# Layer 2's last block by quarters of the tokens, its anchors with the weights held in the array, and the last layer's weights turned in layer 0

## The chip, the cores and the metric

The kernel runs on one core of a Trainium2 chip. The core has a matrix engine (TensorE, PE in the profile; its weight loads are shown apart as PEld), a vector engine (VectorE, DVE), a scalar engine (ScalarE, ACT), GpSimd (POOL) and a queue engine (SyncE, SP), which here issues nearly all of the DMAs. Each engine works through its own queue in order. They meet through semaphores. The metric is the device time of one execution in microseconds (us). The time before is the median of three runs; the profile is of one more execution.

## What is computed

The reference chains four layers over 1024 tokens of 512 features, each as `x = x + ffn(cond(x))`. All is f32.

```python
x = x + _L0_ffn_ref(_L0_cond_ref(x, ...))   # gated FFN with LoRA, then top-2 of 8 LoRA experts
x = x + _L1_ffn_ref(_L1_cond_ref(x, ...))   # adapter pair, then softmax-weighted experts
x = x + _L2_ffn_ref(_L2_cond_ref(x, ...))   # attention over a paged cache, then the block below
x = x + _L3_ffn_ref(_L3_cond_ref(x, ...))   # top-2 experts, then 64 experts, top 16
```

The change rewrites the second half of layer 2, with `x` there the attention's output (called `y2` in the kernel):

```python
def _L2_ffn_ref(x, W, b, A, Bmat, LiMEs):         # A: 512x32, Bmat: 32x512, LiMEs: 8x32
    H = jnp.einsum('btd,od->bto', x, W) + b
    z = jnp.einsum('btd,dr->btr', x, A)
    anchors = jnp.arange(N_GRAM - 1, T, N_GRAM)   # every second token, from token 1
    H_slice = H[:, anchors, :E]
    delta_slice = jnp.einsum('bar,er->bae', z[:, anchors], LiMEs)
    H_scale = jnp.maximum(jnp.max(jnp.abs(H_slice)), EPS)
    d_scale = jnp.maximum(jnp.max(jnp.abs(delta_slice)), EPS)
    logits = ((1.0 - GAMMA) * (H_slice / H_scale) + GAMMA * (delta_slice / d_scale)) / TEMPERATURE
    probs = jax.nn.softmax(logits, axis=-1)
    ...                                           # thresholded and normalised: weights
    p_mix = jnp.einsum('bte,er->btr', jnp.repeat(weights, N_GRAM, axis=1), LiMEs)
    return H + jnp.einsum('btr,ro->bto', z * p_mix, Bmat) * scaling
```

Layer 3 uses, among others, a 512x512 matrix `W` (`base3` in the kernel) and the experts' `B` (`wB3`) in a turned form. Layer 2 uses the product of `A` and `LiMEs` transposed, for which `A` (`A2`) must be turned.

## The kernel before

The 1024 tokens lie in the columns of `x`, a tile of 128 partitions by four chunks of features by 1024 tokens. A block is 128 tokens (eight blocks), a half is 512, a quarter is 256. Every f32 matmul stands as two records in the trace and a transpose on PE as one.

*Order.* The engines' queues come out of a scheduling layer that may move instructions past each other where data allow. `kept(...)` keeps an instruction in program order on its engine. PE's matmuls stand in program order in the parts named here.

*Layer 0* ends (lines 632 to 672) with the down projection: four `Down` objects, one for each half of the tokens `g` and of the outputs `k`, each a list of matmuls `dn` over the inner dimension with VectorE additions `du`, `dp` between (`begin`, `go_on`), then `lora` and `out`. VectorE, POOL and SP have gaps there.

*Layer 2's attention* is `run` (line 1326), a loop of 32 steps `n`. In each step PE makes scores `st` (line 1173), ACT exponentials, PE the weighted values `av` (line 1225). The sums go through `sums` in DRAM: SP writes `sums<-inv` (line 1217) and reads `R<-sums` (line 1218), and VectorE scales `av` by R into `oT` (line 1235). The output projection is the Strassen-like products `wo_one`, `wo_two`, `wo_six` (line 979) over quarters. From `n == 5` on, `end.prepare` (line 1784) builds part of the layer's second half: four PE transposes turn `A2` (`A2Tp`), ACT copies it to `A2T`, and `alp` (line 1794) multiplies it with LiMEs into columns 8 to 15 of `WH`, whose first eight columns are rows of the layer's W. In the last steps the blocks of `y2` are turned on PE (`turn`, `y2T`, line 1812).

*The second half of layer 2* is in `ending` (line 1741). `low` (line 1815) makes z for one half of the tokens: `A2` is held as the weights for 16 matmuls of 128 columns, each block on one of four groups of 32 array columns; VectorE copies it to `zq`. `anchors` (line 1824) makes the logits' two parts `hd`: 128 anchor tokens are the weights (every second column of `y2T`), `WH` (16 columns) streams, eight matmuls a half (two groups of anchors, four chunks of features), and VectorE adds the bias `b16`. `product` (line 1841) makes H for a block: 16 matmuls of 128 columns into one bank `h`. Low and anchors of the first half run at step 30 (lines 1422 to 1424), product of block 0 after step 31 (line 1427), the rest in `layer2` (line 2195). `routing` (line 1855) reduces `hd` to two maxima, takes them over the partitions with the POOL all-reduce `top` (line 1867) and makes the weights `p` on VectorE and ACT. `gains` (line 1904) turns `p` on PE (`pT`), multiplies by LiMEs (`pmix`) and forms `zp = 0.5 z p_mix`. `delta` (line 1928) adds Bmat's product into the open banks of H, 16 matmuls of 128 columns a half, and VectorE adds H to `x`, one block at a time. Between the products `weights_turned` (line 1971) turns layer 3's `base3` (`W3p`, 16 PE transposes, four ACT copies) and `wB3` (`wB3p`, four transposes, one copy), and `fold_scores` (line 1985) multiplies them with router matrices (`qwp`, `qbp`, `fkp`, `gkp`).

*Layer 3* begins with PE's `midp` matmuls (line 53, a helper), which read `x` in order of the blocks. POOL makes sums of weights for its fast products (`Bws`, `W3s`, line 2012). `sums_checked` (line 756) reads the attention's sums back, reduces them on VectorE and over the partitions with POOL's all-reduce `anyone` (line 765), and copies the result to `redo_i` on VectorE; if a sum lies out of its range, a second, general attention would run behind the kernel.

## Time and profile before

| | us |
|---|---|
| runs of before | 1492.9, 1496.06, 1497.18 (median 1496.06) |
| the profiled execution's own time | 1490.35 |
| its span on the core | 1488.6 |
| `av` matmuls (line 1225), busy | 290.8 |
| `st` matmuls against the cache (line 1173), busy | 237.4 |
| `h`, layer 2's product, busy (256 records) | 31.2 |
| the attention's steps, about | 250 to 1350 |
| layer 2's second half, from the last `y2T` to layer 3's first `midp` | 1352.6 to 1389.7 |
| layer 3, to the end | 1389.7 to 1488.6 |

The profiled execution is 5.7 us shorter than the median of the runs, and 1.75 us of it lie around the span. The busy time of a group adds the records' own durations. Matmuls overlap a little, so in a timeline a group's stretch, from its start to the start of the next, is shorter than its busy time. A timeline line gives the start, the busy time, the engine, the line, the operation, what it writes and reads, the shape, how many records, and in brackets the idle time before and what ended it. A line of windows gives, for each stretch, the busy time and the instructions of PE, PEld, DVE, ACT and POOL, then the clock that TensorE was granted (1.00 is full), the DMA engines' share, and GB/s. In the chain of waits each piece has its start, its length and what ran.

### The profile page before, as it was taken

To read this page: it belongs to the slowest core of one execution; us is meant where nothing else is said; L and a number is where in the kernel's file an instruction comes from. 1 tells how busy PE (TensorE), PEld (TensorE's weight loads), DVE (VectorE), ACT (ScalarE), POOL (GpSimd) and SP (SyncE) were. 2 spreads that over 40 slices of the span, in tenths; PEclk is the share of its full clock that TensorE was granted. 3 is DMA by queue.
4 is the path that set the end of the run, shared out by engine and by line. 5 is a ranking of instruction groups with operands and counts; after the bars stand their busy time and mean duration, and the time that the engine had idled before them with its cause. 6 is when DMAs were issued, how large, how long until landed. Compare 5 with 4: busy or idle time off the path is not lost.

```text
span 1488.6 us, 18093 instructions
## 1 busy us (share of the span) xinstructions
PE 1476.6 (99%) x5603; PEld 938.3 (63%) x5603; DVE 1065.6 (72%) x2121; ACT 562.0 (38%) x1422; POOL 856.4 (58%) x876
## 2 busy tenths in 40 slices
PE   9999999999999999999999999999999999999998
PEld 7888787455555655555555555565555555558887
DVE  4665425388888787787778778787878878855475
ACT  1111101044545544454554454454445455431110
POOL 2241104567777777776777777677777777622310
PEclk9999999999999999999999999999999999999999
DMA  7411001213545444564454455345445534433001
GB/s 242 118 44 32 1 1 55 94 36 115 183 148 173 150 119 129 150 183 126 135 152 131 128 158 177 110 135 163 129 125 166 168 106 138 120 104 98 1 9 52
DMA packets 155257, 171.44 MB, mean 115 GB/s; under 512 B 52624, under 2 KB 125776, under 8 KB 155024
## 3 DMA queue, kind: packets, MB, share of 16 engines
q1 hardware_dynamic: 136976, 133.18, 30.0%
q0 software_dynamic: 17056, 36.49, 7.7%
q8 instruction: 47, 0.77, 0.2%
q10 hardware_dynamic: 1120, 0.52, 0.1%
q14 instruction: 58, 0.48, 0.1%
HBM read 129.36 MB, written 40.76 MB: 114 GB/s over the span
## 4 chain that ended last, share of the span: by engine, by line
PE 96%; DVE 2%; ACT 0%; DMA 0%; issue 0%; DVEq 0%; ACTq 0%; SPq 0%
PE st L1173 18%; PE av L1225 18%; PE g L367 9%; PE q_six L979 8%; PE wo_two L979 6%; PE q_one L979 6%; PE q_five L979 6%; PE dn L367 5%; PE wo_six L979 4%; PE wo_one L979 4%; PE eo_l L53 3%; PE z L1761 2%; PE h L1761 2%; PE midp_l L53 1%; PE o L1761 1%; PE gu L367 1%
## 5 line engine op out<-in xcount | busy, mean ns | idle before, releaser
L922 POOL DMA_INDIRECT kn<-in_k_cache,kvrow_k x256 | 272.2, 1063 | 77.1 <-issue 71.2
L922 POOL DMA_INDIRECT vals<-in_v_cache,kvrow_v x256 | 272.3, 1064 | 73.6 <-issue 60.2
L1225 PE MATMUL av<-pT,vals 128*128 128x512 f32 x640 | 290.8, 592 | 0.2 <-DVE oT L1235 0.2
L1177 ACT ACTIVATE pT<-st,hide 128x512 f32<-128x512 f32 x256 | 175.9, 687 | 192.0 <-PE st L1173 178.8
L1173 PE MATMUL st<-qT,kT 128*128 128x512 f32 x512 | 237.4, 596 | 0.0
L1225 PEld LDWEIGHTS av<-pT,vals 128*128 128x128 f32 x640 | 121.4, 190 | 152.7 <-issue 148.3
L1078 POOL TENSOR_TENSOR vq<-q,txq 128x256 f32<-128x256 f32 x128 | 121.1, 976 | 130.6 <-ACT sqq L1052 92.9
L1173 PEld LDWEIGHTS st<-qT,kT 128*128 128x128 f32 x512 | 97.2, 191 | 109.3 <-issue 103.3
L1193 DVE TENSOR_TENSOR part<-pT 128x512 f32<-128x512 f32 x128 | 88.3, 691 | 76.2 <-ACT pT L1177 62.8
L979 PE MATMUL q_one<-q,x 128*128 128x384 f32 x256 | 93.0, 486 | 0.0
L1052 ACT ACTIVATE sqq<-q 128x128 f32<-128x128 f32 x252 | 78.2, 310 | 10.4 <-DVE q L1028 3.8
L979 PEld LDWEIGHTS q_one<-q,x 128*128 128x128 f32 x256 | 48.5, 190 | 39.8 <-issue 14.3
L979 PE MATMUL q_six<-q_s,xs_all 128*128 128x384 f32 x192 | 69.8, 486 | 0.0
L1033 ACT COPY q<-q_one 128x256 f32<-128x256 f32 x32 | 11.9, 372 | 151.9 <-PE q_one L979 133.5
L979 PE MATMUL wo_one<-o,oT 128*128 128x256 f32 x256 | 65.9, 380 | 1.1 <-ACT k L1033 0.8
L1173 PE MATMUL st<-qT,kTn 128*128 128x512 f32 x128 | 65.4, 592 | 0.0
L979 PE MATMUL wo_two<-o_s,os 128*128 128x256 f32 x256 | 60.6, 379 | 0.3 <-DVE os L938 0.3
L1177 ACT ACTIVATE pT<-st,rs 128x512 f32<-128x512 f32 x64 | 44.0, 687 | 38.5 <-PE av L1225 18.5
L979 PEld LDWEIGHTS wo_one<-o,oT 128*128 128x128 f32 x256 | 48.5, 190 | 15.0 <-issue 1.9
L436 POOL TENSOR_TENSOR ws<-wu 128x256 f32<-128x256 f32 (+1 forms) x9 | 6.4, 711 | 86.8 <-DMA wu<-in_WuT 79.8
L1209 ACT COPY rows<-rows 32x32 f32<-32x32 f32 x96 | 20.7, 216 | 92.1 <-DVE rows L1204 91.4
L367 PE MATMUL g<-xs,ws 128*128 128x256 f32 (+1 forms) x240 | 55.1, 379 | 0.0
(461 smaller groups left out, 2838.5 us busy)
## 6 DMA issues: line engine op xcount, KB each, us to landing
turned_new<-qkt SPq DMA_DIRECT2D x120, 160.0 KB
turned_cached<-kt SPq DMA_DIRECT2D x128, 128.0 KB
kT<-turned_cached SPq DMA_DIRECT2D x32, 512.0 KB
R<-sums SPq DMA_DIRECT2D x32, 512.0 KB
qT<-turned_new SPq DMA_DIRECT2D x30, 512.0 KB
q<-in_WqT SPq DMA_DIRECT2D x8, 1024.0 KB
o<-in_WoT SPq DMA_DIRECT2D x8, 1024.0 KB
kn<-in_k_cache,kvrow_k POOLq DMA_INDIRECT x256
```

The lines of the kernel that those rows point to most:

```text
L53: pe.matmul(o, lhsT, rhs, start=start, stop=stop)
L367: pe.matmul(o, lhsT, rhs, start=start, stop=stop, skip_group_check=True)
L922: kept(pool.indirect_dma_start(out=d[:, c, :], out_offset=None, in_=kc if what == "k" else vc, in_offset=bass.IndirectOffsetOnAxis(ap=kvro ...
L979: kept(pe.matmul(o, l[:, c, :], r[:, c, :], start=start and c == 0, stop=c == 1, skip_group_check=True))
L1052: kept(act.activation(sq, S[n][m][:, j, i, :], AF.Square, accum_out=S[n]["ssq"][:, j, col : col + 1]))
L1078: kept(pool.tensor_tensor(to, t[:, b, :, hi : hi + 64], wx[:, b, lo : lo + 64].unsqueeze(2).to_broadcast(list(to.shape)), ALU.mult,))
L1173: kept(pe.matmul(ps, s["kT"][:, c, 4 * j : 4 * j + 4, :] if c < 4 else s["kn"][:, j], s["qT"][:, :, REP * j : REP * (j + 1), :].rearrange( ...
L1177: kept(act.activation(pT[:, c, :, :].rearrange("p i t -> p (i t)"), ps, AF.Exp, **(dict(bias=hide[:, b, c : c + 1]) if c < 4 else dict(bia ...
L1193: kept(dve.tensor_tensor(o, l, r, ALU.add))
L1209: kept(act.copy(rows[0:32, g, :], rows[32 * g : 32 * g + 32, 0, :]))
L1225: kept(pe.matmul(ps, v[:, c, :], pT[:, c, :, :].rearrange("p i t -> p (i t)"), start=c == 0, stop=c == NC - 1, skip_group_check=True,))
L1761: return pe.matmul(o, lhsT, rhs, start=start, stop=stop, skip_group_check=True)
```

## The change

- *Product by quarters.* `product` takes 256 tokens in one matmul instead of 128: 64 matmuls in all for 128. A bank holds two chunks of outputs for a quarter, so each quarter has two banks. Quarter 0 (was: block 0) stands after step 31, the others in `layer2`.
- *Low and anchors once.* Both run once in `layer2` for all tokens and are gone from step 30. `low` has a quarter of the tokens on each group of 32 array columns, 16 matmuls of 256 columns; ACT copies it. `anchors` holds `WH` as the weights, padded with zeros from 16 to 32 columns (a POOL memset), and streams the anchors of a quarter (128 columns at a stride of two) to each column group, 16 matmuls; VectorE copies the result, `low` runs, and one PE transpose turns it.
- *`pmix`* is four matmuls of 128 columns instead of eight of 64. *`delta`* is 16 matmuls of 256 columns, a quarter on each row group, instead of 32 of 128; quarter 3's delta opens its banks, and product adds to them.
- *Turned weights.* `base3`, `wB3` and `A2` are loaded in layer 0 (six SP DMAs), turned by VectorE in blocks of 32x32, and written to DRAM tensors (24 SP DMAs, pieces of 128 bytes that put each block in its place), in three pairs between the `Down` parts. Later `W3` and `wB3T` are loaded from there in the place of `base3` and `wB3`, and `A2T` at step 5 by an SP DMA. All PE transposes of these three, and the six ACT copies, are gone.

In the order of the engines' queues, the changed kernel has: on SP at step 5, `A2T`'s DMA right behind `R<-sums`; on POOL, both groups of `W3s` sums (eight operations) ahead of the all-reduce `anyone`, where before the second group stood behind it; on VectorE, `x<-h` of quarters 0 to 2 (first bank), then `redo_i`, then `x<-h` of the second banks and of quarter 3; on PE, after the last turns, anchors, z, one transpose, the product of quarter 1 and half of 2, `qwp`, `qbp`, `pT`, `pmix`, the other half of quarter 2, delta, half of quarter 3, `fkp`, `gkp`, the other half, `midp`.

```diff
+    late_weights = [
+        (a["base3"][d * P : (d + 1) * P, :], w3T[:, d * P : (d + 1) * P].rearrange("(b i) (q j) -> q i b j", i=32, j=32))
+        for d in range(DC)
+    ]
+    late_weights.append((a["wB3"], wB3T.rearrange("(b i) (q j) -> q i b j", i=32, j=32)))
+    late_weights.append((
+        a["A2"].rearrange("(c p) r -> p c r", p=P), A2T.rearrange("i (c q j) -> q i c j", q=4, j=32)
+    ))
...
+        def weights_turned():
+            for n in range(0, len(late_weights), 2):
+                ts = []
+                for i, (src, _) in enumerate(late_weights[n : n + 2]):
+                    t = w0.tile([P, 2, D], F32, tag=("Ad", "Bg")[i], name=f"late_{n + i}")
...
+                    kept(sp.dma_start(first if len(src.shape) == 2 else first.rearrange("p (c j) -> p c j", j=src.shape[2]), src))
+                    ts.append((t, m))
+                for (_, dst), (t, m) in zip(late_weights[n : n + 2], ts):
+                    kept(dve.transpose(t[:, 1, :m], t[:, 0, :m]))
+                    for q in range(4):
+                        kept(sp.dma_start(dst[q], t[32 * q : 32 * q + 32, 1, :m].rearrange("i (b j) -> i b j", j=32)))
+                yield
...
-        for d in downs:
-            d.go_on()
+        turning = weights_turned()
+        downs[0].go_on()
+        next(turning)
+        downs[1].go_on()
...
         downs[0].go_on()
+        next(turning)
         mids0, route0, mix0, outs0 = experts("l0", ...)[:4]
...
         downs[1].go_on()
+        next(turning)
...
-            if n + 2 == len(steps):
-                end.low(0, bank)
-                end.anchors(0, bank)
         divided(n)
         every(outputs(n))
-        end.product(0, "st", bank)
+        end.product(0, ("st", "st"), bank)
...
-    WH = early.tile([P, DC, 16], F32, tag="WH", name="WH")
+    WH = early.tile([P, DC, 32], F32, tag="WH", name="WH")
+    kept(pool.memset(WH[:, :, 16:32], 0.0))
...
     def prepare(bank, room):
-        pt = bank("mm", [P, D], "A2Tp")
-        for c in range(DC):
-            kept(pe.transpose(pt[:32, c * P : (c + 1) * P], A2[:, c, :], ident))
         A2T = room([32, D], "A2T")
-        kept(act.copy(A2T, pt[:32]))
+        kept(sp.dma_start(A2T, late_turned[2]))
...
+    def low(bank):
+        ps = bank("mm", [P, NT // 4], "z2")
         for c in range(DC):
-            for j in range(HB):
-                b = g * HB + j
-                mmq(ps[slot(j), :], A2[:, c, :], Y2T[0][:, c, b * P : (b + 1) * P], c == 0, c == DC - 1)
-        dve.tensor_copy(zq[:, g, :], ps)
+            for q in range(4):
+                mmq(ps[slot(q), :], A2[:, c, :], Y2T[0][:, c, quarter(q)], c == 0, c == DC - 1)
+        act.copy(zq, ps)
+
+    def anchors(bank, meanwhile):
+        ps = bank("mm", [P, P], "hdT")
+        for c in range(DC):
+            for q in range(4):
+                mmq(ps[slot(q), :], WH[:, c, :], Y2T[0][:, c, q * NT // 4 + 1 : (q + 1) * NT // 4 : 2], c == 0, c == DC - 1)
+        hdT = L3.w3.tile([P, P], F32, tag="hdT", name="hdTs")
+        dve.tensor_copy(hdT, ps)
+        meanwhile()
+        ps = bank("mm", [P, NA, 32], "hd")
+        pe.transpose(ps.rearrange("p q e -> p (q e)"), hdT, ident)
+        dve.tensor_tensor(hd, ps[:, :, 0:16], b16.unsqueeze(1).to_broadcast([P, NA, 16]), ALU.add)
...
+    def product(q, tags, bank, at=range(2), begun=False):
+        for i, tag in zip(at, tags):
+            ps = H[q, i] if begun else bank(tag, [P, 2, NT // 4], f"h_{q}_{i}")
+            for o in range(2):
+                for c in range(DC):
+                    mmq(
+                        ps[:, o, :], W["2"][:, c, (2 * i + o) * P : (2 * i + o + 1) * P], Y2T[0][:, c, quarter(q)],
+                        not begun and o == 0 and c == 0, begun and c == DC - 1,
+                    )
+            H[q, i] = ps
...
+    def delta(tags, bank):
+        for i, tag in enumerate(tags):
+            H[3, i] = bank(tag, [P, 2, NT // 4], f"h_3_{i}")
+        for i in range(2):
+            for o in range(2):
+                for q in range(4):
+                    at = (2 * i + o) * P
+                    mmq(H[q, i][:, o, :], Bm[slot(q), at : at + P], zp[slot(q), :], q == 3 and o == 0, q < 3)
+
+    def added(q):
+        for i in range(2):
+            t = x[:, 2 * i : 2 * i + 2, quarter(q)]
+            dve.tensor_tensor(t, H[q, i], t, ALU.add)
...
-        L3.base = load("base3", [P, DC, D], chunks(a["base3"]))
+        L3.W = load("W3", [P, DC, D], chunks(late_turned[0]))
...
-        L3.wB = load("wB3", [P, D], a["wB3"])
+        L3.wBT = load("wB3T", [P, DC, P], chunks(late_turned[1]))
...
-    def layer2(y2, bank, held=lambda: None, do=range(NB)):
+    def layer2(y2, bank, do=range(NB)):
         for b in do:
             turn(y2, b, bank)
...
+        anchors(bank, lambda: low(bank))
         where = ["mm"]
+        folding = fold_scores(lambda tag, shape, name: bank(where[0], shape, name))
+        if (0, 0) not in H:
+            product(0, ("st", "st"), bank)
+        product(1, ("st", "av"), bank)
         routing()
+        product(2, ("av",), bank)
+        next(folding)
         gains(bank)
+        product(2, ("mm",), bank, range(1, 2))
+        delta(("mm", "mm"), bank)
+        for q in range(3):
+            added(q)
         where[0] = "st"
+        product(3, ("mm",), bank, range(1), begun=True)
+        next(folding, None)
+        product(3, ("mm",), bank, range(1, 2), begun=True)
+        added(3)
```

More of the change, by code (lines that the diff above doesn't have):

```diff
@@ L67, in forward @@
     x = xpool.tile([P, DC, NT], F32, tag="x", name="x")
+    w3T, wB3T, A2T = (
+        nc.dram_tensor(n, shape, F32, kind="Internal").ap()
+        for n, shape in (("w3_turned", (D, D)), ("wB3_turned", (D, P)), ("A2_turned", (32, D)))
+    )
[7 more added lines that the diff above has]
+    ))
+    late_turned = w3T, wB3T, A2T
     c0 = ExitStack()
@@ L564, in forward @@
         w11 = const.tile([P, 136], F32, tag="w11", name="w11")
+        def weights_turned():
[3 more added lines that the diff above has]
+                    t = w0.tile([P, 2, D], F32, tag=("Ad", "Bg")[i], name=f"late_{n + i}")
+                    m = math.prod(src.shape[1:])
+                    first = t[:, 0, :m]
+                    kept(sp.dma_start(first if len(src.shape) == 2 else first.rearrange("p (c j) -> p c j", j=src.shape[2]), src))
[5 more added lines that the diff above has]
+                yield
         def ranks_to_ranks(wb1T):
@@ L741, in end_of @@
                 lambda shape, name: ww.tile(shape, F32, tag="q7", name=name),
-                lambda shape, name: ww.tile(shape, F32, tag="qs", name=name), room, chunks, mm, in_order,
+                lambda shape, name: ww.tile(shape, F32, tag="qs", name=name), room, chunks, mm, late_turned, in_order,
             )
@@ L788, in forward @@
                 lambda shape, name: ww.tile(shape, F32, tag="q7", name=name),
-                lambda shape, name: ww.tile(shape, F32, tag="qs", name=name), room, chunks, mm,
+                lambda shape, name: ww.tile(shape, F32, tag="qs", name=name), room, chunks, mm, late_turned,
             )
@@ L1741, in ending @@
 def ending(
-    tc, a, out, x, ident, bias3, experts, early, tile_of_w2, tile_of_aw, room, chunks, mm, kept=lambda i: i
+    tc, a, out, x, ident, bias3, experts, early, tile_of_w2, tile_of_aw, room, chunks, mm, late_turned, kept=lambda i: i
 ):
@@ L1780, in ending @@
     kept(sp.dma_start(b16[:, 0:8], a["b8"].partition_broadcast(P)))
-    zq = early.tile([P, TG, P], F32, tag="zq", name="zq")
+    zq = early.tile([P, NT // 4], F32, tag="zq", name="zq")
     hd = early.tile([P, NA, 16], F32, tag="hd", name="hd")
     def prepare(bank, room):
-        pt = bank("mm", [P, D], "A2Tp")
-        for c in range(DC):
-            kept(pe.transpose(pt[:32, c * P : (c + 1) * P], A2[:, c, :], ident))
         A2T = room([32, D], "A2T")
-        kept(act.copy(A2T, pt[:32]))
+        kept(sp.dma_start(A2T, late_turned[2]))
         yield
@@ L1813, in turn, with quarter @@
         (act.copy if b % 2 else dve.tensor_copy)(Y2T[0][:, :, b * P : (b + 1) * P], ps)
-    def low(g, bank):
-        ps = bank("mm", [P, P], f"z2_{g}")
+    def quarter(q):
+        return slice(q * NT // 4, (q + 1) * NT // 4)
+    def low(bank):
+        ps = bank("mm", [P, NT // 4], "z2")
         for c in range(DC):
-            for j in range(HB):
-                b = g * HB + j
-                mmq(ps[slot(j), :], A2[:, c, :], Y2T[0][:, c, b * P : (b + 1) * P], c == 0, c == DC - 1)
-        dve.tensor_copy(zq[:, g, :], ps)
-    def anchors(g, bank):
-        ps = bank("mm", [P, 2, 16], f"hd_{g}")
-        for i in range(2):
-            t0 = (2 * g + i) * 2 * P
-            for c in range(DC):
-                mm(ps[:, i, :], Y2T[0][:, c, t0 + 1 : t0 + 2 * P : 2], WH[:, c, :], c == 0, c == DC - 1)
-        dve.tensor_tensor(
-            hd[:, 2 * g : 2 * g + 2, :], ps, b16.unsqueeze(1).to_broadcast([P, 2, 16]), ALU.add
-        )
+            for q in range(4):
[12 more added lines that the diff above has]
+        dve.tensor_tensor(hd, ps[:, :, 0:16], b16.unsqueeze(1).to_broadcast([P, NA, 16]), ALU.add)
     H = {}
@@ L1839, in shifted @@
             kept(act.activation(x[:, c, :], x[:, c, :], AF.Identity, bias=bcol[:, c : c + 1]))
-    def product(b, tag, bank):
-        ps = bank(tag, [P, DC, P], f"h_{b}")
-        for o in range(DC):
-            for c in range(DC):
-                mmq(
-                    ps[:, o, :], W["2"][:, c, o * P : (o + 1) * P], Y2T[0][:, c, b * P : (b + 1) * P],
-                    o == 0 and c == 0, False,
-                )
-        H[b] = ps
+    def product(q, tags, bank, at=range(2), begun=False):
[6 more added lines that the diff above has]
+                        not begun and o == 0 and c == 0, begun and c == DC - 1,
+                    )
+            H[q, i] = ps
     sm = early
@@ L1911, in gains @@
         act.copy(pT, pt[:8].rearrange("p i t -> p (i t)"))
-        pm = bank("mm", [P, TG, 64], "pmix")
-        for g in range(TG):
-            for j in range(HB):
-                b = g * HB + j
-                mmq(pm[slot(j), g, :], Li, pT[:, b * 64 : (b + 1) * 64], g == 0, True)
-        zp = L3.w3.tile([P, TG, P], F32, tag="zp", name="zp")
+        pm = bank("mm", [P, P], "pmix")
+        for q in range(4):
+            mmq(pm[slot(q), :], Li, pT[:, q * P : (q + 1) * P], True, True)
+        zp = L3.w3.tile([P, NT // 4], F32, tag="zp", name="zp")
         dve.scalar_tensor_tensor(
-            zp.rearrange("p g (t two) -> p g t two", two=2),
-            zq.rearrange("p g (t two) -> p g t two", two=2),
+            zp.rearrange("p (t two) -> p t two", two=2),
+            zq.rearrange("p (t two) -> p t two", two=2),
             0.5,
-            pm.unsqueeze(3).to_broadcast([P, TG, 64, 2]),
+            pm.unsqueeze(2).to_broadcast([P, P, 2]),
             ALU.mult,
@@ L1926, in gains @@
         Z["zp"] = zp
-    def delta(g):
+    def delta(tags, bank):
         zp, Bm = Z["zp"], L3.Bm
-        for o in range(DC):
-            for j in range(HB):
-                mmq(H[g * HB + j][:, o, :], Bm[slot(j), o * P : (o + 1) * P], zp[slot(j), g, :], False, True)
-        for j in range(HB):
-            b = g * HB + j
-            t = x[:, :, b * P : (b + 1) * P]
-            dve.tensor_tensor(t, H[b], t, ALU.add)
+        for i, tag in enumerate(tags):
+            H[3, i] = bank(tag, [P, 2, NT // 4], f"h_3_{i}")
+        for i in range(2):
+            for o in range(2):
+                for q in range(4):
+                    at = (2 * i + o) * P
[4 more added lines that the diff above has]
+            dve.tensor_tensor(t, H[q, i], t, ALU.add)
     def open3(w3, ex_sm):
@@ L1969, in copied @@
         return t
-    def weights_turned(bank):
-        L3.W = L3.w3.tile([P, DC, D], F32, tag="W3", name="W3")
-        for o in range(DC):
-            ps = bank("mm", [P, DC, P], f"W3p_{o}")
-            for d in range(DC):
-                pe.transpose(ps[:, d, :], L3.base[:, d, o * P : (o + 1) * P], ident)
-            copied(None, None, ps.rearrange("p c d -> p (c d)"), L3.W[:, o, :])
-            yield
-        ps = bank("mm", [P, DC, P], "wB3p")
-        for o in range(DC):
-            pe.transpose(ps[:, o, :], L3.wB[:, o * P : (o + 1) * P], ident)
-        L3.wBT = copied([P, DC, P], "wB3T", ps)
     def fold_scores(bank):
@@ L2193, in last @@
             sp.dma_start(out[o * P : (o + 1) * P, tok], t)
-    def layer2(y2, bank, held=lambda: None, do=range(NB)):
+    def layer2(y2, bank, do=range(NB)):
         for b in do:
             turn(y2, b, bank)
-        for g in range(TG):
-            if g or len(do) > HB:
-                low(g, bank)
-                anchors(g, bank)
+        anchors(bank, lambda: low(bank))
         where = ["mm"]
-        def free(tag, shape, name):
-            return bank(where[0], shape, name)
-        turning, folding = weights_turned(free), fold_scores(free)
-        for b in range(HB):
-            if b not in H:
-                product(b, "av" if b == HB - 1 else "st", bank)
-                next(turning, None)
+        folding = fold_scores(lambda tag, shape, name: bank(where[0], shape, name))
+        if (0, 0) not in H:
+            product(0, ("st", "st"), bank)
+        product(1, ("st", "av"), bank)
         routing()
+        product(2, ("av",), bank)
+        next(folding)
         gains(bank)
-        product(HB, "av", bank)
-        next(turning, None)
-        delta(0)
+        product(2, ("mm",), bank, range(1, 2))
+        delta(("mm", "mm"), bank)
+        for q in range(3):
+            added(q)
         where[0] = "st"
-        for b in range(HB + 1, NB):
-            product(b, "mm", bank)
-            for _ in turning:
-                pass
-            next(folding, None)
-        delta(1)
+        product(3, ("mm",), bank, range(1), begun=True)
+        next(folding, None)
+        product(3, ("mm",), bank, range(1, 2), begun=True)
+        added(3)
     def layer3(bank, between=lambda: None):
@@ L2265, in ending @@
     return SimpleNamespace(
-        prepare=prepare, load_w2=load_w2, load_aw=load_aw, turn=turn, low=low, anchors=anchors,
+        prepare=prepare, load_w2=load_w2, load_aw=load_aw, turn=turn,
         product=product, shifted=shifted, open3=open3, layer2=layer2, layer3=layer3,
```

## Prediction

> **What bounds it now.** I read the busy shares first, then the chain of waits, then TensorE's timeline where the change touches it, then the queues that feed those places.

> ```profile
> PE 1476.6 (99%) x5603; PEld 938.3 (63%) x5603; DVE 1065.6 (72%) x2121; ACT 562.0 (38%) x1422; POOL 856.4 (58%) x876
> ```

> ```profile
> PE 96%; DVE 2%; ACT 0%; DMA 0%; issue 0%; DVEq 0%; ACTq 0%; SPq 0%
> ```

> TensorE (PE) is busy for 99% of the span and 96% of the chain. So the sum is: PE time that goes, less PE time that comes, less new PE idle. An f32 matmul is two records, a transpose one; since records overlap I take a group's cost from its start to the next start.

> The parts that are rewritten, and rows for what replaces them:

> ```profile
> 1309.53 0.82 PE L1761 MATMUL z<-y2T,A 128*32 128x128 f32 x6
> ...
> 1313.46 0.66 PE L53 MATMUL hd<-WH,y2T 128*128 128x16 f32 x5 [0.59 <-issue]
> 1313.97 5.38 PE L1173 MATMUL st<-qT,kT 128*128 128x512 f32 x8
> ```

> ```profile
> 1349.48 1.03 PE L979 MATMUL wo_two<-o,os 128*128 128x256 f32 x4
> 1350.34 1.03 PE L979 MATMUL wo_six<-o_s,oT 128*128 128x256 f32 x4
> ...
> 1374.70 3.84 PE L1761 MATMUL h<-y2T,WT 128*128 128x128 f32 x32
> 1378.38 0.60 PE L1982 MATMUL wB3p<-ident,wB 128*128 128x128 f32 x4
> ...
> 1400.48 1.03 PE L1761 MATMUL fp<-AwT,W 128*128 128x256 f32 x4
> 1401.35 1.03 PE L1761 MATMUL fp<-sums,W 128*128 128x256 f32 x4
> ```

> The reader is to see: half of `low` and `anchors` between two attention steps, 1309.53 to 1313.97, with PE idle 0.59 inside; a block of `product`, 32 records of 128 columns in 3.68 us (0.115 each); and records of 256 columns at 0.86/4 and 0.87/4, mean 0.2165.

> **What goes from PE.** The stretch at 1309.53: 4.44. Its second half in layer 2: z 0.34 + 1.30, hd 1.95, together 3.59. Product: 256 records; its stretches in the timeline add up to 30.0. The 16 transposes `W3p` and 4 `wB3p`: 2.53. `delta`: 2.21. `pmix`: 0.36 (8 records of 64 columns at 0.045). `A2Tp` at step 5: 0.44 (495.58 to 496.02). Three idles of layer 2, before wo_one 0.31, wo_two 0.26 (both behind the wait for R, which the longer first quarter, 32 × 0.2165 = 6.93 from 1340.30 to 1347.2, covers) and pT 0.19: 0.76. Sum 44.3.

> **What comes on PE.** Product: 128 records × 0.2165 = 27.7. `low`: 32 records of 32 rows × 256 columns; the nearest rows are layer 0's td, 88 such records from 166.93 to 171.82, 0.0556 each: 1.78. `anchors`: 32 records of 32 rows × 128 columns at stride 2; nothing like it is in the trace; below, z (26 in 1.02, unit stride): 1.25; above, td at its full 0.0556: 1.78; I take 1.5, as the columns are z's and only the stride is new. One transpose 0.12. `pmix`, 8 records of 128 columns: qbp's 8 take 0.33. `delta`: 32 records from 0.0556 (td) to 0.0675 (g<-tgm, 8 in 0.54): 1.8 to 2.2, taken 2.0. Idles: `hdT` is copied by DVE while `low` runs, 1.8 of cover for a copy of some 0.3 and its hand-overs, taken 0.15; `pmix` stands right behind pT, so PE waits for ACT's copy, 0.57 with hand-overs 0.85. With 0.8 at midp (below) the sum is 35.2.

> **Step 5, a new wait.** `prepare` no longer makes A2T on PE but fetches it over SP's queue, behind R<-sums, while `alp` keeps its place on PE:

> ```profile
> 496.02 4.46 PE L1225 MATMUL av<-pT,vals 128*128 128x512 f32 x10
> 500.41 1.05 PE L1794 MATMUL alp<-LiT,A2T 32*128 32x8 f32 x8
> ```

> ```profile
> 499.14 0.32 SPq L1217 DMA_DIRECT2D sums<-inv  x1
> 500.66 0.35 SPq L1218 DMA_DIRECT2D R<-sums  x1
> 501.05 2.09 SPq L1128 DMA_DIRECT2D turned_cached<-kt  x4
> ```

> ```profile
> 1338.35 1.35 DMA sums<-inv
> ...
> 1339.77 3.81 DMA R<-sums
> ```

> SP waits at 500.66 until sums<-inv has landed, so A2T (64 KB) is issued at some 501.05, where now turned_cached starts. PE reaches alp at 500.41 - 0.44 = 499.97 and waits, and all st matmuls of step 6 stand behind alp on PE. The DMA's time is bounded by the nearest rows: 1.52 from issue to release (sums<-inv here, 499.14 to 500.66), landing at 502.57, idle 2.6; and 3.81 (R<-sums, 512 KB, in the chain), landing at 504.86, idle 4.9. I take 4.9: 64 KB in rows of 2 KB behind R on the same rings is nearer to R than to the small write. Behind A2T on SP the four turned_cached issues come 0.35 later; they serve step 7, so nothing waits. ACT's copy of A2T goes.

> Sum: 44.3 - 35.2 - 4.9 = **4.2 us gained**.

> **The clock.** After the stretch with z and hd the granted clock falls:

> ```profile
> 1314.00:1316.00 2.00, 2.00 (x5) 0.96 (x5) 0.20 (x2) 0.06 (x1) 0.00 (x0) 0.53 1.04 403
> 1316.00:1318.00 2.00, 2.00 (x4) 0.72 (x4) 0.00 (x0) 0.98 (x2) 0.00 (x0) 0.62 1.04 377
> ```

> (third to last: clock). The eight st matmuls take 5.21 there and 3.44 elsewhere: 1.77 lost. The change removes that stretch, but PE's new idle before alp may bring a drop of its own. I set the one against the other, net 0; the bounds are +1.77 (the old drop goes, none comes) and -1.77 (the old one stays by other causes, a new one comes).

> [...]

> **Hidden, costed at nothing.** In layer 0 VectorE turns five 128x512 tiles (0.70 each, as STREAM_TRANSPOSE partT 0.706) and one 128x128: 3.7 us in DVE's idles 178.60 to 191.19, 212.76 to 224.67 (11.90) and 233.3 to 242.55. PE's dn matmuls cover them; SP is idle from 132.6 to 243.22, so 6 loads and 24 stores (8 a pair, 0.65 issue each as the two kTn in 1.19 show, 5.2 a pair) fit, the last pair from 234.4 to 239.6, ahead of q<-in_WkT at 243.22. If that cover went, q<-in_WkT would be late, then q_s on DVE (251.42) and eo's add (256.45) behind it; PE needs that bank at 264.8: some 7.7 us of slack. The stores go out in pieces of 128 bytes; the DMA share is near zero there and W3 is wanted 1100 us later. W3 and wB3T take base3's and wB3's place in the load queue with the same bytes. `low`'s copy moves from DVE to ACT, idle there.

> **POOL, and midp.** Now the second group of W3s runs behind the second all-reduce; after the change both stand ahead of it.

> ```profile
> 1359.14 0.37 POOL L1867 PARTITION_ALL_REDUCE top<-big  x1 [25.89 <-DVE big L1863]
> 1366.23 1.40 POOL L2012 TENSOR_TENSOR W3s<-W 128x256 f32<-128x256 f32 x2 [6.71 <-ACT m L1893]
> ...
> 1379.24 0.38 POOL L765 PARTITION_ALL_REDUCE anyone<-some  x1 [5.83 <-issue]
> 1386.32 1.40 POOL L2012 TENSOR_TENSOR W3s<-W 128x256 f32<-128x256 f32 x2 [6.70 <-ACT gk L1968]
> ```

> After an all-reduce POOL is idle 6.7 before its next arithmetic, and 5.83 the other way (1373.41 to 1379.24). In the times of before: layer 2's turns end at 1355.6 (product's quarter is 2.2 longer), hd is ready near 1360, `top` ends near 1360.7; 6.7 later, 1367.4, 16 operations start (0.69 to 0.72, 11.3 together), end 1378.7; 5.83 gives 1384.5; `anyone` 0.38, `redo_i`, and the add x<-h_0_1 (0.62) behind it on DVE: 1385.8. PE: pT 1369.6, pmix 1370.5, product to 1374.3, delta to 1376.3, product 1379.8, fold 1380.8, product 1384.3 (midp begins at 1389.69 today). midp's first two matmuls use x rows that are ready, the third, at 1385.0, waits for x<-h_0_1: the 0.8 above. Routing, from top to p, is 3.17 shorter, since ACT's Exp `m` no longer stands behind W3p's copies; p is ready at 1366.5, before PE wants it.

> **Rivals.**
> (1) *A2T lands early, and the clock drop only goes.* For: R's 3.81 is for 512 KB, A2T is an eighth. Against: it shares the rings with R. Gain 4.2 + 2.3 + 1.77 = 8.3: 1487.8. Chance 0.22.
> (2) *Slower: POOL holds midp.* PE's third midp matmul waits, through redo_i, on `anyone`. For: 16 elementwise operations and two idles of some 6 us stand ahead in one queue. Against: the rows at hand are 0.69 to 0.77. At 0.976 each (vq<-q,txq, same shape) the 16 take 4.3 longer: no gain, 1496. At 1.175 (the largest xs<-x) 7.5 longer: 4.2 - 7.5 = -3.3: 1499.4. It decides above 4.2, that is from 0.97 an operation. Chance 0.12.
> (3) *256 columns bring nothing per column*: h stays 30.0, as two records of 0.117. For: h comes with a weight load of 128 columns either way, 0.14 to 0.19, hidden behind 0.2165. Against: wo and fp. Gain 4.2 - 2.3 = 1.9: 1494.2. Chance 0.16.
> The forecast itself: 0.50.

> **The numbers.** The sum is against the profiled execution, 1490.35 (span 1488.6): 1486.2 there. That execution lies 5.7 under the median of three runs, 1496.06, which spread over 4.3; I carry the difference over: 1496.06 - 4.2 = **1491.9**. Its own range: A2T 2.6, clock ±1.77, anchors and delta ±0.5: 1487.3 to 1494.2, and with 1.5 for the spread of a median, 1486 to 1496. The range reaches to the other cases, 1485.0 to 1499.5: 1487.8 less half the runs' spread below, rival 2 above.
> What can't be told from no change is 0.3%, 4.5 us: faster is under 1491.6. Forecast: half faster, half same, 0.25 + 0.24, slower 0.01; rival 1: 0.19 and 0.03; rival 2: half slower 0.06, half same 0.06; rival 3: 0.01 faster, 0.13 same, 0.02 slower; 0.45, 0.46, 0.09, of which I move 0.05 from same to slower, as the runs of before differ by 4.3 among themselves: 0.45, 0.41, 0.14.

> **What would show it.** PE idle of 2.6 to 4.9 before alp near 500, released by A2T's DMA; the clock in the windows behind it and near 1310; h at 0.2165 a record; W3p and wB3p gone; p ready before PE's pT; `anyone` ending near 1384.9 (what comes before layer 2 cancels: 4.44 + 0.44 - 4.9), and PE's wait at the third midp matmul under 1 us. The forecast falls if that wait is over 5, if alp doesn't wait at all, or if a layer-0 gap appears before eo's bank near 264.8.

## The result and the profile after

The changed kernel took 1493.97 us (median of 14 runs, 1488.16 to 1497.01) beside 1495.61 us for the kernel before (14 runs, 1492.68 to 1498.42): a ratio of 0.9989, 95% interval 0.9978 to 0.9999, that is 0.1 to 3.3 us faster with 1.6 in the middle. Repeated later beside fresh runs of before, the ratio was 1.0003 (0.9994 to 1.0013). So the change brings next to nothing, while some 7 us of TensorE's busy time have gone. The profiled execution took 1490.86 us with a span of 1489.0, against 1488.6 before.

The page of the changed kernel, busy shares and the chain of waits by engine:

```profile
PE 1469.2 (99%) x5380; PEld 926.4 (62%) x5380; DVE 1066.2 (72%) x2125; ACT 559.3 (38%) x1417; POOL 853.0 (57%) x877
```

```profile
PE 90%; issue 4%; DVE 3%; POOL 1%; another core or an unknown queue 1%; ACT 0%; DMA 0%; SPq 0%; DVEq 0%; POOLq 0%; ACTq 0%
```

PE's busy time fell by 7.4 us and the span did not. The chain's shares do not measure what was lost: once PE waits at all, everything that led up to the wait counts, so 90% instead of 96% is not 6% of the time. They say where to look. Up to the start of layer 3 the chain's long detours from PE end at three waits: `st` at 403.50 (0.39 us of idle), `alp` at 505.94 (5.45) and `midp` at 1389.22 (0.50). The long wait is `alp`'s, in step 5.

Step 5 on PE, then on SP's queue, in the changed kernel's timeline:

```profile
505.94 1.84 PE L1823 MATMUL alp<-LiT,A2T 32*128 32x8 f32 x8 [5.45 <-issue]
507.71 5.48 PE L1207 MATMUL st<-qT,kT 128*128 128x512 f32 x8
513.03 1.02 PE L1207 MATMUL st<-qT,kTn 128*128 128x512 f32 x2
```

```profile
501.20 0.34 SPq L1252 DMA_DIRECT2D R<-sums  x1
501.58 0.43 SPq L1819 DMA_DIRECT2D A2T<-A_turned  x1
```

`alp` waits 5.45 us; A2T is issued at 501.58 and used at 505.94, 4.36 later. Then two groups run slow: alp takes 1.77 from start to next start (0.98 before, from 500.41) and the eight st records 5.32 (3.54 before):

```profile
501.39 3.70 PE L1173 MATMUL st<-qT,kT 128*128 128x512 f32 x8
504.93 1.02 PE L1173 MATMUL st<-qT,kTn 128*128 128x512 f32 x2
```

The windows of the changed kernel, where the third number from the end is the granted clock, say why:

```profile
500.00:502.00 2.00, 0.48 (x2) 0.00 (x0) 1.81 (x4) 0.00 (x0) 1.39 (x3) 1.00 0.24 55
502.00:504.00 2.00, 0.00 (x0) 0.00 (x0) 0.77 (x3) 0.00 (x0) 1.69 (x2) 1.00 0.87 227
504.00:506.00 2.00, 0.06 (x1) 0.09 (x1) 0.00 (x0) 0.00 (x0) 1.39 (x3) 0.63 1.00 349
506.00:508.00 2.00, 2.00 (x9) 1.98 (x10) 0.00 (x0) 0.18 (x1) 1.61 (x2) 0.50 0.43 145
508.00:510.00 2.00, 2.00 (x3) 0.88 (x3) 0.00 (x0) 0.18 (x2) 0.95 (x1) 0.50 0.76 229
510.00:512.00 2.00, 2.00 (x4) 0.74 (x3) 0.00 (x0) 1.00 (x2) 0.00 (x0) 0.67 0.26 98
512.00:514.00 2.00, 2.00 (x6) 0.87 (x5) 0.74 (x2) 1.57 (x3) 0.00 (x0) 1.00 0.00 0
```

The clock falls to 0.50 late in the wait, near 504.5, and stays there until 511.3, 5.4 us after `alp` and 3.6 after the first `st` have begun. The two groups lose 0.79 + 1.78 = 2.57 us by it.

Layer 2's second half on PE, and POOL beside it:

```profile
1343.46 7.07 PE L1792 MATMUL h<-y2T,WT 128*128 128x256 f32 x32
1350.37 1.03 PE L1013 MATMUL wo_one<-o,oT 128*128 128x256 f32 x4
...
1372.55 0.60 PE L1944 MATMUL pT<-ident,p 128*8 128x128 f32 x4
1373.81 0.42 PE L1792 MATMUL pmix<-pTs,Li 8*32 8x128 f32 x8 [0.66 <-ACT pTs L1946]
1374.16 3.72 PE L1792 MATMUL h<-y2T,WT 128*128 128x256 f32 x16
1377.81 2.01 PE L1792 MATMUL h<-zp,Bm 32*128 32x256 f32 x32
...
1387.88 0.84 PE L53 MATMUL midp_l<-wmr,x 128*128 128x200 f32 x4
1389.22 5.00 PE L53 MATMUL midp_l<-wmr,x 128*128 128x200 f32 x28 [0.50 <-DVE x L1975]
```

```profile
1363.48 0.38 POOL L1902 PARTITION_ALL_REDUCE top<-big  x1 [27.06 <-DVE big L1898]
1370.93 1.41 POOL L2034 TENSOR_TENSOR W3s<-W 128x256 f32<-128x256 f32 x2 [7.07 <-issue]
...
1388.00 0.38 POOL L799 PARTITION_ALL_REDUCE anyone<-some  x1 [5.85 <-issue]
```

A quarter of the product takes 6.91 us for 32 records (0.216 each). From its start to midp's first matmul it is 44.42 us, against 49.39 before: 4.97 gained, less the 0.50 that midp waits for `x`, behind `anyone`. Before:

```profile
1340.30 3.74 PE L1761 MATMUL h<-y2T,WT 128*128 128x128 f32 x32
...
1389.69 5.68 PE L53 MATMUL midp_l<-wmr,x 128*128 128x200 f32 x32
```

How much later PE stood than in the first profile of before, read at the last wo_six of a step:

| stretch, in times of before | later by |
|---|---|
| start to step 4 (486.1) | +0.44 |
| step 5 into 6 (520.0): alp's wait and the half clock | +7.66 |
| steps 6 to 29 (1294.8) | +1.39 |
| step 30 (1329.1): z and hd gone, and the half clock behind them | -6.32 |
| product's first part, a quarter for a block (1350.3) | +2.04 |
| the rest of layer 2, to midp (1389.7) | -7.02 |
| midp to PE's last group | +0.52 |
| sum | -1.29 |

Behind PE's last group the end of the program, from the last `x` add to the end of the span, took 4.93 before and 6.62 after. That is how a gain of 1.3 on PE shows as a span 0.4 longer. Over all the profiles here this end takes 4.72 to 5.44 in the four without the turning in layer 0 (before twice, and two of the experiments) and 5.71 to 6.94 in the nine with it. The traces do not show what runs there, so whether the turning lengthens it stays open.

### The profile page after: what moved, and what is told of

It is laid out like the page before. It is cut to its first block, busy times and chain, and to the rows that moved or that the text cites. A ratio compares the mean times of both kernels' runs of the same rounds, so it can differ in the third digit from the quotient of the medians.

```text
span 1489.0 us, 17706 instructions
## 1 busy us (share of the span) xinstructions
PE 1469.2 (99%) x5380; PEld 926.4 (62%) x5380; DVE 1066.2 (72%) x2125; ACT 559.3 (38%) x1417; POOL 853.0 (57%) x877
## 4 chain that ended last, share of the span: by engine, by line
PE 90%; issue 4%; DVE 3%; POOL 1%; another core or an unknown queue 1%; ACT 0%; DMA 0%; SPq 0%; DVEq 0%; POOLq 0%; ACTq 0%
PE st L1207 18%; PE av L1259 17%; PE g L381 9%; PE q_six L1013 8%; PE q_one L1013 5%; PE q_five L1013 5%; PE wo_two L1013 5%; PE dn L381 5%; PE wo_one L1013 3%; PE wo_six L1013 3%; PE eo_l L53 3%; PE z L1792 2%; PE o L1792 1%; PE midp_l L53 1%; PE gu L381 1%
## 5 line engine op out<-in xcount | busy, mean ns | idle before, releaser
L956 POOL DMA_INDIRECT vals<-in_v_cache,kvrow_v x256 | 269.0, 1051 | 73.6 <-issue 59.9
```

Source lines behind the costliest of these rows:

```text
L956: kept(pool.indirect_dma_start(out=d[:, c, :], out_offset=None, in_=kc if what == "k" else vc, in_offset=bass.IndirectOffsetOnAxis(ap=kvro ...
```

## Experiments

All ratios are to the kernel before, with a 95% interval. The first four kernels, the next four and the last three each ran on one chip beside their own runs of before.

**A2T fetched a step earlier.** The tile that it uses is free from step 3 on.

```diff
-            if n == 5:
-                prepared = end.prepare(bank, lambda shape, name: wk.tile(shape, F32, tag="xs", ...))
-            next(prepared, None)
             every(mix(n, 1))
...
             if n == 4:
                 end = end_of(kept)
+                prepared = end.prepare(bank, lambda shape, name: wk.tile(shape, F32, tag="xs", ...))
+                next(prepared)
```

> A2T is fetched at the end of step 4 instead of behind R<-sums in step 5; alp keeps its place on PE. Theory: in the changed kernel's profile the wait of alp cost 5.45 us of PE idle and then 2.57 us of half clock (alp 0.79 and the eight st 1.78 longer). Both go: PE idle before alp under 0.2, the clock at 1.00 from 498 to 514, and about 8.0 us less than the changed kernel, 9.6 less than before, ratio 0.9936. Rival A: the wait only hid another one (R, the next step's scores), which now shows: PE idle of some us appears elsewhere in steps 5 and 6, and the gain on the changed kernel is under 3 us, ratio above 0.997. Rival B: the half clock near 505 comes from something else than the idle (DMA load): then 5.5 less than the changed kernel, ratio 0.9953, and the dip stays.

Measured: 1482.06 beside 1490.58, ratio 0.9950 (0.9937 to 0.9964). PE's timeline of this run:

```profile
500.38 1.05 PE L1822 MATMUL alp<-LiT,A2T 32*128 32x8 f32 x8
501.36 3.70 PE L1207 MATMUL st<-qT,kT 128*128 128x512 f32 x8
```

No idle before alp, st at its usual 3.54, the clock at 1.00 from 498 to 514; at the last wo_six of this stretch PE stands 0.03 ahead of before, where the changed kernel stood 8.10 behind. Neither rival holds: nothing took the wait's place, and the half clock went with it. The ratio expected, 0.9936, lies just below the interval: 0.9950 is 5.8 us under the changed kernel's 0.9989, not 8.0. The comparison on one chip, below, gives 7.7.

**A2T fetched in step 5, but ahead of R.**

```diff
         kept(sp.dma_start(here.rearrange("(c a) -> c a", a=32), r[:, 1, :]))
+        between()
         kept(sp.dma_start(R.rearrange("p j i t -> p (j i t)"), here.partition_broadcast(P)))
...
-            inverted(n, some(w_ops))
+            inverted(n, some(w_ops), lambda: next(prepared, None) if n == 5 else None)
```

> A2T is fetched in step 5 between sums<-inv and R<-sums, so about 1.6 us earlier than in the changed kernel. Theory: it lands 1.5 to 4.4 us after its issue near 500.0 (4.36 in the changed kernel, from 501.58 to 505.94), so PE idles 1.0 to 3.9 us before alp; the half clock began 4.0 us after the start of the idle in the changed kernel, so here it does not come: alp back at 1.05, 4.1 to 7.0 us less than the changed kernel. Rival: any idle of over half a us brings the drop, as before near 1314 after an idle of 0.59: the clock dips, and 2.57 of the loss stays, 1.5 to 4.4 us less than the changed kernel.

Measured: ratio 0.9970 (0.9961 to 0.9980). PE's timeline and windows of this run:

```profile
501.78 1.02 PE L1823 MATMUL alp<-LiT,A2T 32*128 32x8 f32 x8 [1.96 <-DVE xs_all L972]
502.73 5.40 PE L1207 MATMUL st<-qT,kT 128*128 128x512 f32 x8
```

```profile
503.00:504.00 1.00, 1.00 (x3) 0.46 (x3) 0.00 (x0) 0.13 (x2) 0.70 (x2) 0.89 0.90 281
504.00:505.00 1.00, 1.00 (x2) 0.34 (x1) 0.00 (x0) 0.58 (x1) 0.69 (x2) 0.50 1.06 377
...
507.00:508.00 1.00, 1.00 (x4) 0.51 (x3) 0.00 (x0) 0.69 (x1) 0.70 (x2) 0.90 0.46 147
```

The idle shrank to 1.96 as the theory had it: A2T, issued at 499.27, was used 2.51 later. (`xs_all`, which the line names as the releaser, is not what `alp` needs: in the first experiment `alp` begins ahead of it, at 500.38 against 500.96.) But the half clock came all the same, 0.50 from about 503.8 to 507.2, and st took 5.23 instead of 3.54. My theory of the clock fell here: in this run 1.96 us of idle with 0.95 of alp behind it were followed by the drop. The rival's outcome came, but its rule, any idle of over half a us, does not hold either: the clock stayed at 1.00 behind pmix's idle of 0.66, and behind one of 1.24 at 17.85 in layer 0 of the first experiment.

**Low and anchors of the first half moved into layer 2, in the kernel before.**

```diff
-            if n + 2 == len(steps):
-                end.low(0, bank)
-                end.anchors(0, bank)
...
-            if g or len(do) > HB:
-                low(g, bank)
-                anchors(g, bank)
+            low(g, bank)
+            anchors(g, bank)
```

> The kernel before with low and anchors of the first half moved from step 30 into layer 2, in their old form; nothing else. Theory: the stretch of narrow records with its 0.59 idle is what brought the half clock near 1314 to 1317.5; without it st x8 of step 31 takes 3.44 instead of 5.21, and the idle goes: 0.59 + 1.77 = 2.4 us less than before, ratio 0.9984, less what the routing gets later. Rival: the drop comes from the DMA load of that time (share 1.02 to 1.06) and stays: about 0.6 less than before, ratio 0.9996, and the clock still dips between 1308 and 1320.

Measured: ratio 0.9998 (0.9989 to 1.0007). At step 30 the half clock was gone (1.00 from 1304 to 1322) and PE gained 6.3 us on before: the 4.44 of the block that moved away, with its idle of 0.59, and 1.9 of half clock. By midp only 1.44 was left. PE's timeline in layer 2 of this run, and one of its windows:

```profile
1348.23 2.06 PE L53 MATMUL hd<-WH,y2T 128*128 128x16 f32 x16
1350.21 1.08 PE L1758 MATMUL z<-y2T,A 128*32 128x128 f32 x32
1351.23 3.26 PE L53 MATMUL hd<-WH,y2T 128*128 128x16 f32 x16
1354.32 6.92 PE L1758 MATMUL h<-y2T,WT 128*128 128x128 f32 x42
```

```profile
1352.00:1353.00 1.00, 1.00 (x6) 1.00 (x7) 0.04 (x1) 0.00 (x0) 0.00 (x0) 0.50 0.00 0
```

Two runs of 16-column matmuls now stand together, and the half clock (0.50 from 1351.67 to 1358.50) has moved there with them: the second takes 3.09 instead of 1.98, and 42 product records 6.76 instead of some 4.8, though PE is never idle and no DMA is running. So the drop of before at 1314 goes with this block, not with the DMA load of that time. One half of it alone, as it stands in layer 2 of before (hd, z and hd, 3.3 us from 1354.52), leaves the clock at 1.00 (1354 to 1364). The changed kernel's anchors stream 128 columns, and the clock is 1.00 there (1356 to 1376).

**The changed kernel without the turning in layer 0.**

```diff
-        turning = weights_turned()
         downs[0].go_on()
-        next(turning)
         downs[1].go_on()
...
-        L3.W = load("W3", [P, DC, D], chunks(late_turned[0]))
+        L3.W = load("W3", [P, DC, D], chunks(a["base3"]))
...
-        kept(sp.dma_start(A2T, late_turned[2]))
+        kept(sp.dma_start(A2T, a["A2"].rearrange("(i b) r -> i (b r)", i=32)))
```

> The changed kernel without the six loads, six VectorE transposes and 24 stores in layer 0; W3, wB3T and A2T are read from the untouched weights with the same bytes, so layer 3 and the routing of layer 2 compute with weights that are not turned. Theory: the turning is hidden: within 0.5 us of the changed kernel, and dn, q_s and eo begin at the same times to 0.1 us. Rival: the stores in pieces of 128 bytes or the DVE time delay steps behind layer 0 (the changed kernel's PE is 0.44 late near 421 and 1.0 more from 842 to 1295): 0.5 to 1.5 us less than the changed kernel, and that lag is gone.

Measured: ratio 0.9995 (0.9986 to 1.0005), between the changed kernel's two results (0.9989 and 1.0003). PE's groups of layer 0 keep their lengths (dn 4.32 for 20 records in both), and steps 6 to 29 drift by 0.77 here. On PE the turning is hidden; in the whole time the interval leaves room for some 1.5 us, and the end of the program takes 4.72 here, the least of all. The rival's lag in steps 6 to 29 is not shown to be the turning's: the drift of 0.77 without it and 1.39 with it is within what profiles of one kernel differ by (below).

**alp four times over**, on top of the first experiment, so that A2T is in time:

```diff
-        for c in range(DC):
+        for c in [c for _ in range(4) for c in range(DC)]:
             kept(pe.matmul(ps[:, c, :], A2T[:, c * P : (c + 1) * P], LiT, start=True, stop=True))
```

> e1_early with alp's four matmuls (8 columns each, 0.98 us for the four) issued four times over, with the same result; A2T is there in time, so PE never idles. Theory: matmuls that stream so few columns count as idle for the clock: the clock falls within some 4 us, as it did in e2_between after 1.96 of idle and 0.95 of alp, and st x8 behind takes over 5 us instead of 3.5. Cost over e1_early: 3 x 0.98 = 2.9 for the matmuls and 1.7 to 2.6 for the clock, 4.6 to 5.5. Rival: only idle brings the drop, narrow matmuls don't: the clock stays at 1.00 and the cost is 2.9.

Measured: ratio 0.9987 (0.9977 to 0.9996), 0.0037 or 5.5 us over the first experiment. PE's timeline and windows:

```profile
500.63 4.54 PE L1822 MATMUL alp<-LiT,A2T 32*128 32x8 f32 x32
505.10 6.21 PE L1207 MATMUL st<-qT,kT 128*128 128x512 f32 x8
```

```profile
502.00:503.00 1.00, 1.00 (x12) 1.00 (x11) 0.97 (x4) 0.00 (x0) 0.94 (x1) 1.00 0.41 78
503.00:504.00 1.00, 1.00 (x9) 1.00 (x8) 0.17 (x1) 0.00 (x0) 0.71 (x1) 0.68 0.59 205
504.00:505.00 1.00, 1.00 (x6) 1.00 (x6) 0.00 (x0) 0.00 (x0) 0.70 (x2) 0.50 0.67 248
```

PE is busy for the whole of every window (the first number after the comma), and the clock falls to 0.50 some 2.7 us after the narrow matmuls begin (500.63 to 503.36); st takes 6.05. So in this run 32 records of eight columns, with PE busy throughout, were followed by the same drop to 0.50 as 5.45 us of idle in the changed kernel. This run can't tell the few columns from the 32 rows that alp fills; that it is the columns is my guess from `hd`, which fills all 128 rows and streams 16 columns and stood ahead of the drop at 1351.67 above. No run here shows it by itself.

**pT ahead of qwp and qbp, and redo_i on POOL**, on top of the first experiment:

```diff
-        next(folding)
-        gains(bank)
+        gains(bank, lambda: next(folding))
...
         act.copy(pT, pt[:8].rearrange("p i t -> p (i t)"))
+        meanwhile()
         pm = bank("mm", [P, P], "pmix")
...
-        dve.tensor_copy(redo_i, anyone)
+        pool.tensor_copy(redo_i, anyone)
```

> e1_early with two more edits: in layer 2 pT is turned before qwp and qbp, so that ACT's copy runs under them, and redo_i is written by POOL instead of VectorE. Theory: PE's idle of 0.66 before pmix goes, and midp can wait no more for anyone: 0.7 less than e1_early, ratio to before 0.9945, PE idle before pmix and before midp under 0.1. Rival: the time comes back behind, because p or zp is late or POOL's copy holds up xs: within 0.2 of e1_early, with a new idle on PE between 1360 and 1400.

Measured: ratio 0.9931 (0.9918 to 0.9945). PE's timeline of this run:

```profile
1366.19 0.60 PE L1943 MATMUL pT<-ident,p 128*8 128x128 f32 x4
1366.72 1.07 PE L1791 MATMUL qwp<-W,Wq 128*32 128x512 f32 x8
1367.61 0.40 PE L1791 MATMUL qbp<-wB3T,Wq 128*32 128x128 f32 x8
1367.94 0.42 PE L1791 MATMUL pmix<-pTs,Li 8*32 8x128 f32 x8
```

The wait before pmix is gone and so is midp's, though `anyone` ends at 1383.56, 1.35 after midp's start at 1382.21. From the last wo_six to midp it is 31.70 us instead of 32.34.

**A2 turned on PE as before, in the changed kernel.**

```diff
+        pt = bank("mm", [P, D], "A2Tp")
+        for c in range(DC):
+            kept(pe.transpose(pt[:32, c * P : (c + 1) * P], A2[:, c, :], ident))
         A2T = room([32, D], "A2T")
-        kept(sp.dma_start(A2T, late_turned[2]))
+        kept(act.copy(A2T, pt[:32]))
```

> The changed kernel with A2 turned on PE in step 5 as in the kernel before (four transposes, a copy by ACT) instead of fetched. Theory: the whole of the alp wait is the DMA's: PE idle before alp under 0.2, no half clock, 0.44 more than e1_early for the transposes, 7.5 less than the changed kernel, ratio to before 0.9953. Rival: part of the loss sits elsewhere in the steps behind (the changed kernel drifts by 1.4 from step 6 to step 30): under 6 less than the changed kernel.

Measured: ratio 0.9952 (0.9935 to 0.9968), the same as A2T fetched early. No idle before alp, no half clock. The 0.44 between the two is below what these runs can tell apart.

**The kernel before once more, and the three main kernels beside each other.**

> The kernel before once more, for its trace alone. The changed kernel and its relatives lose 0.8 to 1.4 us against the first profile of before between steps 6 and 30, where nothing differs. Theory: that is scatter of single executions (waits of 0.2 to 0.5 for qT): this profile differs from the first by as much. Rival: it is the change's (other places in memory): this profile agrees with the first to 0.3 us there.

Between steps 6 and 29 this profile of before loses 1.19 us against the first one (from 0.91 ahead to 0.28 behind), as much as the changed kernel's 1.39. So two profiles of one kernel differ as much, and the drift need not be the change's. The half clock behind z and hd is there too, and longer:

```profile
1314.81 6.65 PE L1173 MATMUL st<-qT,kT 128*128 128x512 f32 x8
1321.29 1.02 PE L1173 MATMUL st<-qT,kTn 128*128 128x512 f32 x2
```

6.48 for st in place of 5.21: in before, too, this loss varies between executions (the last section has the lengths).

> The changed kernel again, beside e1_again and e6_again on one chip, so that the three are compared by the same runs of before. By the steps of the traces: ratio to before 0.9989 as first measured (0.9978 to 0.9999), and PE's wait before alp of 5 to 6 us with the half clock behind it, as in the first profile. Rival: the wait is scatter of one execution: it is under 3 us here.

> A2T fetched at the end of step 4. Theory: 8.0 us less than a2_after (idle 5.45, half clock 2.57), so a ratio 0.0054 lower, near 0.9935. Rival: only 5.5 less, 0.0037 lower, as the medians of the first call gave: then part of what the trace shows at step 6 comes back as waits in the steps behind.

> e1_early with pT ahead of qwp and qbp and redo_i on POOL. Theory: 0.64 less than e1_again (from the last wo_six to midp 31.70 instead of 32.34 us), ratio 0.0004 lower. Rival: the 0.0019 between the first two calls is real, 2.8 us: then something behind midp gains too.

Measured: 1.0003 (0.9994 to 1.0013), 0.9951 (0.9938 to 0.9965) and 0.9938 (0.9924 to 0.9952). The changed kernel's alp waited 6.28 this time, with alp and st again at half clock:

```profile
505.51 1.84 PE L1823 MATMUL alp<-LiT,A2T 32*128 32x8 f32 x8 [6.28 <-issue]
507.28 6.45 PE L1207 MATMUL st<-qT,kT 128*128 128x512 f32 x8
```

Fetching A2T early is worth 0.0052, 7.7 us, by the medians; by single profiles, steps 5 and 6 take 8.1 us less in the first pair and 9.9 in this one. The last edits are 0.0013 more, 1.9 us. Of this the two profiles show 0.63 ahead of midp and 0.49 behind it (22.91 from the first midp to the second instead of 23.40); the intervals overlap, so the rest is not shown.

## Why the prediction came out as it did

The direction came out in the first comparison, the size did not: 4.2 us forecast, 1.6 measured, and no change in the repetition. That 1493.97 lies within the prediction's own range of 1486 to 1496 says little, as that range is ten us wide. The layer-2 part came out for the reasons given; step 5 did not.

- *The sum over layer 2 held.* In the times of before, midp was to begin at 1384.3 and wait 0.8, a gain of 4.6; measured 4.97 less 0.50. The product's records are 0.216 (0.2165 reckoned), delta 1.94 (2.0), pmix's wait 0.66 by the profile (0.85 with hand-overs). Set back by the 3.16 by which PE is late at the product's start, p is ready at 1365.6 (1366.5 reckoned), PE reaches pT at 1369.4 (1369.6) and `anyone` ends at 1385.2 (1384.9). (The terms of the sum alone give 4.2 for this part, the times 4.6. And the lower end of the wide range, rival 1 less half the runs' spread of 4.3, is 1485.7, not 1485.0.)
- *What was costed at nothing* held on PE: `dn` keeps its lengths, and SP issues q<-in_WkT at 243.06 (243.22 before), not late.
- *The rival of 256 columns that bring nothing* is out: 0.216 for 256 columns against 0.115 for 128.
- *The rival of POOL* is out: its sixteen operations took 11.2 us together (11.3 reckoned, from 1370.93 to 1382.16), and midp waited 0.50 to 0.51.
- *The rival of an early A2T* is what the first experiment made of the kernel, but the change itself does not do it.
- *alp's wait* was reckoned at 2.6 to 4.9, and 4.9 taken. Measured: 5.45, 6.04 and 6.28. The upper bound came from the landing of R, 3.81 after its issue; A2T, an eighth of R's bytes but queued behind it, took 4.36 from its issue to its use, and 2.51 when it was issued ahead of R. So R's 3.81 was no upper bound for a transfer that stands behind R.
- *The step that failed is the clock's:* "I set the one against the other, net 0", with 1.77 as the most that a new drop would cost. What went at step 30 was indeed some 1.8 (6.32 gained there, 4.44 of it the matmuls). What came at step 5 was 2.57, and 3.54 in the second profile of the changed kernel, since the half clock covered alp as well as st and lasted two and three times as long as the one that went (6.83 and 10.24 us against 3.41, last section). Together with the wait, the stretch from 486 to 520 cost 7.66 where 4.46 had been reckoned. The rest is 0.44 and 1.39 of drift, no more than two profiles of before differ by, and 1.69 behind PE's end, whose cause stays open.

The sentence that the old drop "goes" with the stretch was right. In the old form (`hd` with 16 columns) the drop moves along with the anchors into layer 2, where the clock is 0.50 from 1351.67 to 1358.50; in the new form (128 columns), in the same place, it does not come (1.00 from 1356 to 1376). That the few columns of `hd` are the reason is a guess from these two, and from the alp of eight columns four times over.

## What to carry to other kernels

Where the matrix engine sets the end, a DMA that replaces a little work of that engine must be issued so early that it can't be late: saving 0.44 us of transposes in step 5 cost 8 us, and issuing the same DMA a step earlier made the whole change worth 7 us. Look at the granted clock behind a wait on that engine too: behind the waits of 1.96 to 6.28 us at `alp` the half clock cost another 1.7 to 3.5 us here. And look at it behind long runs of matmuls with few columns: here 4.5 us of eight columns, and 6.1 us of hd, z and hd, were followed by the same 0.50 with no idle at all. The version with A2T fetched early, pT first and redo_i on POOL is the fastest here, at 0.9931 and 0.9938 of before.

## What was not expected of the hardware

```profile
14.49 1.13 PE L381 MATMUL gu<-x,wg 128*128 128x256 f32 x4 [1.88 <-issue]
```

The stretches at half clock between PE's first and last matmul, over all these profiles, from windows of 0.1 us (the profiles that are not listed have none):

| profile | from, to | us |
|---|---|---|
| before | 1314.11, 1317.52 | 3.41 |
| before once more | 1313.97, 1320.80 | 6.83 |
| changed | 504.50, 511.33 | 6.83 |
| changed once more | 502.61, 512.85 | 10.24 |
| without the turning | 502.44, 512.68 | 10.24 |
| A2T ahead of R | 503.79, 507.20 | 3.41 |
| old block in layer 2 | 1351.67, 1358.50 | 6.83 |
| alp four times over | 503.36, 510.19 | 6.83 |
| pT ahead, layer 0 | 15.72, 19.13 | 3.41 |

Three last 3.41 us, four 6.83 and two 10.24; the kernel before had 3.41 in one execution and 6.83 in the other, the changed kernel 6.83 and 10.24. So the price of a drop varied from execution to execution, in the changed kernel from 2.57 to 3.54. In the two drops worked out here the price is near half of that part of the stretch in which PE has work: 505.94 to 511.33 is 5.39, half of it 2.70, and 2.57 was lost; 503.79 to 507.20 is 3.41, half of it 1.70, and 1.69 was lost. The fall came 2.7 us after the first alp with alp four times over (500.63 to 503.36), 4.0 after the start of the idle in the changed kernel (500.49 to 504.50) and 4.6 after the first z in before (1309.53 to 1314.11). From the next st to full speed it took 3.6 in before (1313.97 to 1317.52) and 6.0 in before once more (1314.81 to 1320.80). In between the clock was 0.50.
